# Grid values transposed by TensorE in front of their rescaling, and the split middle chunk of the down projection in two 12-bit parts

## The chip, the cores and the metric

The kernel runs on one core of one Trainium2 chip. The metric is the device time of one execution in microseconds (us). The kernel before takes 656.72 us, the median of three runs (656.42 to 659.26). TensorE (PE) multiplies matrices and transposes, VectorE (DVE), ScalarE (ACT) and GpSimd (POOL) work element by element, and SyncE (SP) issues the DMAs. Each engine takes its instructions in program order and waits for the others on semaphores.

## The reference

The input `x` has 4 batches of 2048 tokens with 256 values. Everything is float32. Per batch:

```python
xn = layernorm(x)
Q, K, V = xn @ Wq.T + bq, xn @ Wk.T + bk, xn @ Wv.T + bv
Q, K = l2_norm(Q), l2_norm(K)                  # over the tokens
tailor = 1 / (L + einsum('bnc,bc->bn', Q, sum(K) + 1e-6))
s = xn + gamma * (sum(V) + Q (K.T V)) * tailor # linear attention
gate, up = q(xn) @ q(w_gate).T, q(xn) @ q(w_up).T
h = silu(gate) * up                            # 704 values per token
g = silu(q(h) @ q(w_down).T)
out = x + s * g
```

`q` is a blockwise 4-bit quantization and its inverse: in each block of 16 neighbouring values the scale is the largest magnitude divided by 6, each value divided by its scale is rounded to the grid 0, 0.5, 1, 1.5, 2, 3, 4, 6 (with sign), and multiplied by the scale again. A grid value fits 16 bits exactly, and a grid value times its scale needs float32.

## The kernel before

**Tiling.** The 8192 tokens are 32 groups of 256. A group lies on 128 partitions with two tokens (`t` = 0, 1) on each. The attention uses that all it needs of a batch is the Gram matrix of `xn` with a column of ones: `gram_step` (L325) adds a group to it, after the eighth group of a batch `attention` turns it into a 256x256 matrix `M`, and `attend` (L509) multiplies each group's transposed tokens with it.

**One group's way through the feed-forward part.** `normalize` (ScalarE, L300) makes `xn`. The blocks' scales are found by VectorE (L152, L161, L165), `over` divides by them (L178), `short` (ScalarE, L211) makes 16-bit patterns and `on_grid` (VectorE, L221) rounds these to the grid. So far the tokens are on the partitions; the matmuls need the features there. So the 16-bit grid values are transposed, and multiplied afterwards by scales that are transposed as well: `turn_scales` transposes the scales of h of one group and of x of another on TensorE (L394), ScalarE evicts them, one DMA writes them to DRAM (`there`) and another reads them back with each scale repeated for its block (`se`, 960 KB). `turn_q` (L413) transposes the grid values, with a DMA from SBUF to SBUF. `rescale_x` (L417) and `rescale_h` (L427) multiply the two into `xqt` and `hqt`. The first five groups of x go another way: they are rescaled first and transposed as float32 by TensorE (`turn_xq`, L362).

`gate_up` (L440) multiplies `xqt` with the gate and up weights, 2 tokens x 3 column chunks; ScalarE evicts the halves (`si`, `up`) and GpSimd multiplies them to `h`. `down` (L467) multiplies `hqt` with `wdt`.

**The 11 chunks of h.** The 1408 values of a partition (704 of each token) are 11 chunks of 128, so that the middle one holds 64 values of the first token and 64 of the second. `down` uses it twice, once for each token, against weights whose other half is zero: 6 + 6 matmuls of 128x128 by 256 columns.

**The order.** It is written out by hand. A loop over `s` = 3 to 30 issues in one step: `gate_up` of group s+1 in three pieces with `gram_step(s+3)` between them, the scales of h of group s-1, `rescale_x(s+2)`, `turn_xn(s+3)`, `down(s-3)`, `turn_scales`, `attend(s-7)`, the grid values of h of group s-1 and x of group s+3 with their `turn_q`, `rescale_h(s-2)`, stores, and `normalize(s+4)`. The attention of a batch is a generator: each `turn()` issues its next piece (L573 and L618 to L693). Behind the loop the last groups are finished with less to put between them. PSUM has eight banks: two `tp` (transposes and the attention), two `gu`, two `od` (down projection and the attention), `at`, `gram`.

**Queues.** All DMAs of a step stand in SP's queue: load of x, reload of x, `there`, `se`, the transposes of h and x, and the store.

Of the kernel before, what the change touches and what calls it, by code (L numbers as in the profile page):

```python
# [8 lines left out]
F32 = mybir.dt.float32  # L9
BF16 = mybir.dt.bfloat16  # L10
F16 = mybir.dt.float16
AF = mybir.ActivationFunctionType
ALU = mybir.AluOpType
# [6 lines left out]
ONE = 2.0**-14  # L20
TO_512 = 2.0**32
DOWN = 1.0 - 3 * 2.0**-24


@with_exitstack
def kernel(
# [22 lines left out]
    nc = tc.nc  # L49
    B, C, L = x.shape  # L50
    FF = w_gate.shape[0]
    P = 128
    T = 2
# [18 lines left out]
    alg = ctx.enter_context(tc.tile_pool(name="alg", bufs=1))  # L72
    ps_tp = ctx.enter_context(tc.tile_pool(name="ps_tp", bufs=2, space=bass.MemoryType.PSUM))
    ps_gu = ctx.enter_context(tc.tile_pool(name="ps_gu", bufs=2, space=bass.MemoryType.PSUM))
    ps_od = ctx.enter_context(tc.tile_pool(name="ps_od", bufs=2, space=bass.MemoryType.PSUM))
    dram = ctx.enter_context(tc.tile_pool(name="dram", bufs=2, space=bass.MemoryType.DRAM))
# [71 lines left out]
    nc.scalar.activation(small.tile([P, 1], F32, tag="warm", name="warm"), ident[:, 0:1], AF.Silu)  # L148

# [215 lines left out]


    scales, spread_sc, turned = {}, {}, {}

# [40 lines left out]

    def turn_q(kind: str, n: int, q: bass.AP):  # L410
        F = q.shape[1]
        qt = tok.tile([P, F // P, P], F16, tag=f"qt{kind}", name=f"qt_{kind}{n}", bufs=2 if kind == "h" else 1)
        nc.sync.dma_start_transpose(qt, q)  # L413
        turned[kind, n] = qt

    def rescale_x(n: int, key: int):
        nc.vector.tensor_tensor(  # L417
            xqt_tile(n),
            turned.pop(("x", n)).rearrange("p g t -> p (g t)"),
            spread_sc[key][:, NIC:, :].rearrange("p g t -> p (g t)"),  # L420
            ALU.mult,
        )

    def rescale_h(n: int):
        ht = tok.tile([P, HF], F32, tag="hqt", name=f"hqt_{n}", bufs=2)
        hqt[n] = ht.rearrange("p (g t) -> p g t", t=P)
        nc.vector.tensor_tensor(  # L427
            ht,
            turned.pop(("h", n)).rearrange("p g t -> p (g t)"),
            spread_sc[n][:, 0:NIC, :].rearrange("p g t -> p (g t)"),  # L430
            ALU.mult,
        )

# [26 lines left out]
    hqt = {}  # L460

    def down(n: int):
        od = ps_od.tile([P, T, L], F32, tag="od", name=f"dn_{n}")
        half = NIC // T
        for t in range(T):
            for i in range(half + 1):
                nc.tensor.matmul(  # L467
                    od[:, t, :],
                    hqt[n][:, t * half + i, :],
                    wdt[:, t * (half + 1) + i, :],  # L470
                    start=(i == 0),
                    stop=(i == half),
                )
        hqt.pop(n)
        return od
# [70 lines left out]
    def attention(b: int):  # L546
# [18 lines left out]
        yield  # L565
        yield
        xs = []
        for i, (pool, tag) in enumerate(
            ((ps_od, "od"), (ps_tp, "tp"), (ps_tp, "tp"), (ps_od, "od"))
        ):  # L570
# [9 lines left out]
            xs.append(ps)  # L580
        yield
        yield
# [62 lines left out]
        for c in range(KC):  # L645
# [6 lines left out]
            )  # L652


        pts = []
        for t in range(KC):
# [9 lines left out]
            pts.append(ps)  # L666
        yield
        yield
# [48 lines left out]

    wdt = const.tile([P, NIC + 1, L], F32, tag="wdt", name="wdt")

    def turn_d(wdz):  # L720
        half = NIC // T
        H = P // 2
        ends = small.tile([P, KC, P], F32, tag="ends", name="ends", bufs=1)
        w3 = wdz.rearrange("p (t f) -> p t f", t=KC)
        nc.scalar.copy(ends[:, :, 0:H], w3[:, :, FF - H : FF])
        nc.scalar.copy(ends[:, :, H:P], w3[:, :, 0:H])
        nc.gpsimd.memset(wdt[H:P, half, :], 0.0)
        nc.gpsimd.memset(wdt[0:H, half + 1, :], 0.0)
        for i in range(0, NIC - 1, 2):
            tp = ps_tp.tile([P, 512], F32, tag="tp", name=f"tp_d{i}")  # L730
            at = [i + k if i + k < half else i + k + 2 for k in range(2)]
            for k in range(2):
                f0 = at[k] * P if at[k] < half else (at[k] - half - 2) * P + H
# [4 lines left out]
            if at[1] == at[0] + 1:  # L738
                evict_over_one(wdt[:, at[0] : at[0] + 2, :].rearrange("p i n -> p (i n)"), tp)
            else:  # L740
                for k in range(2):
                    evict_over_one(wdt[:, at[k], :], tp[:, k * L : (k + 1) * L])
            yield
        tp = ps_tp.tile([P, 512], F32, tag="tp", name="tp_d")
        for t in range(KC):
            nc.tensor.transpose(tp[:, t * P : (t + 1) * P], ends[:, t, :], ident)
        evict_over_one(wdt[0:H, half, :], tp[0:H, 0:L])
        evict_over_one(wdt[H:P, half + 1, :], tp[H:P, 0:L])
        yield
# [104 lines left out]
    turn_xq(4, rounded(s_x, tx))  # L854
    turn_q("h", 0, on_grid(h_state, th))
    gate_up(3, 0, *chunks[1])
# [14 lines left out]
    turn_scales(1)  # L871
    turn_q("h", 1, on_grid(h_state[1], th))
    turn_q("x", 5, on_grid(s_x, tx))
    load_x(9)
    rescale_h(0)
    normalize(6)
    moments = statistics(7, 8)
# [13 lines left out]
    for s in range(3, N - 1):  # L891
# [100 lines left out]
    gate_of(n - 2, od)  # L992
    turn_q("h", n, on_grid(h_state, th))
    rescale_h(n - 1)
    for i in range(4):
# [5 lines left out]
    rescale_h(n)  # L1001
    gate_of(n - 1, od)
# [55 lines left out]
```

## Time and profile before

| | |
|---|---|
| time, median of 3 runs | 656.72 us (656.42 to 659.26) |
| the profiled execution's own time | 656.78 us |
| its span, first to last instruction | 655.0 us |
| TensorE busy | 635.2 us, 97% of the span |
| VectorE, ScalarE, GpSimd busy | 398.1, 286.8, 289.3 us |
| DMA moved | 74.17 MB, mean 113 GB/s |
| DMA transposes | 32 of h (4.65 us median on the queue), 27 of x (4.70 us) |

A row of a group of instructions has the line of the kernel, the engine, the operation, what it writes and reads by the program's names, the shape, the count, then busy time in us and the mean of one in ns, then the engine's idle time just before them and who ended it. A row of the timeline has start and length in us. "PEld" is TensorE's weight load, which overlaps its passes ("PE"). A float32 matmul of the program leaves two loads and two passes in the trace. The lengths of passes hold the drain of the array, and neighbours overlap, so a pass's cost is the distance between two starts. "issue" is time in which an engine waited for nothing that the profile shows.

### The profile page before, as it was taken

The numbers are of one execution on the slowest core, as the hardware profiler recorded it, in microseconds if no ns is written. First come the engines' busy times: TensorE is split into PE (matmuls) and PEld (weight loads), VectorE is DVE, ScalarE is ACT, GpSimd is POOL, SyncE is SP. The second block draws the span as 40 slices with busy tenths as digits, with TensorE's granted clock in tenths as the row PEclk, the third lists the DMA queues.
The fourth block names the chain that finished last, engine by engine and source line by source line (L and its number), as shares of the span: only waits on it lengthen the run. The fifth ranks groups of instructions, "written<-read, shape, count | busy, mean of one in ns | idle before, by whom it ended". The sixth has DMA issues, their size and how long they took to land.

```text
span 655.0 us, 7910 instructions
## 1 busy us (share of the span) xinstructions
PE 635.2 (97%) x2484; PEld 435.2 (66%) x2486; DVE 398.1 (61%) x707; ACT 286.8 (44%) x701; POOL 289.3 (44%) x545
## 2 busy tenths in 40 slices
PE   4899999999999999999999999999999999999997
PEld 2455666666766666667766666776666766666886
DVE  6777584958574555747554565836757554566632
ACT  2557745343444444334534534444444444433230
POOL 5656362452535363172644525264263625336132
PEclk9999999999999999999999999999999999999999
DMA  9200578876778487857488877748868784885882
GB/s 220 90 18 0 74 126 111 108 110 71 113 112 130 122 138 139 142 59 115 116 139 142 112 109 133 113 108 140 134 77 127 114 112 108 123 124 80 143 197 83
DMA packets 86230, 74.17 MB, mean 113 GB/s; under 512 B 64076, under 2 KB 70444, under 8 KB 86188
## 3 DMA queue, kind: packets, MB, share of 16 engines
q1 hardware_dynamic: 85916, 73.40, 67.2%
q8 instruction: 20, 0.33, 0.2%
q10 hardware_dynamic: 272, 0.26, 0.1%
q14 instruction: 22, 0.18, 0.1%
HBM read 48.30 MB, written 10.27 MB: 89 GB/s over the span
## 4 chain that ended last, share of the span: by engine, by line
PE 95%; ACT 2%; DVE 1%; DMA 1%; POOL 1%; issue 0%; SPq 0%; DVEq 0%; ACTq 0%; POOLq 0%
PE gu L440 46%; PE dn L467 25%; PE at L509 8%; PE gram L325 6%; PE px L573 2%; PE tp_xn L342 2%; PE pm L659 1%; PE pa L638 1%; DMA wgu_n<-in_L_ffn_w_up_dram 1%; PE tp_sc L394 1%; PE tp_xq L362 0%; ACT xn L300 0%; PE pM L693 0%; PE pq L623 0%; PE tp_d L735 0%
## 5 line engine op out<-in xcount | busy, mean ns | idle before, releaser
L440 PE MATMUL gu<-wgu,xqt 128*128 128x512 f32 (+1 forms) x768 | 314.1, 557 | 2.2 <-ACT xqt L312 2.2
L453 POOL TENSOR_TENSOR h<-si,up 128x256 f32<-128x256 f32 (+1 forms) x192 | 154.8, 811 | 296.3 <-ACT up L451 296.3
L440 PEld LDWEIGHTS gu<-wgu,xqt 128*128 128x128 f32 x768 | 142.4, 190 | 134.2 <-issue 104.3
L467 PE MATMUL dn<-wdt,hqt 128*128 128x256 f32 x768 | 171.0, 379 | 0.0
L449 ACT ACTIVATE si<-gu 128x256 f32<-128x256 f32 (+1 forms) x192 | 70.7, 368 | 203.0 <-PE gu L440 201.1
L467 PEld LDWEIGHTS dn<-wdt,hqt 128*128 128x128 f32 x768 | 144.1, 190 | 19.0
L417 DVE TENSOR_TENSOR xqt<-qt_x,se 128x512 f32<-128x512 f16 x27 | 25.7, 951 | 153.7 <-DMA qt_x<-t_x 153.7
L451 ACT COPY up<-gu 128x256 f32<-128x256 f32 (+1 forms) x192 | 67.8, 353 | 0.0
L178 DVE SCALAR_TENSOR_TENSOR y_h<-h,inv_h 128x1408 f32<-128x1408 f32 x32 | 57.5, 1796 | 5.9 <-ACT t_h L211 4.9
L325 PEld LDWEIGHTS gram<-xn 128*128 128x128 f32 x256 | 44.2, 194 | 25.3 <-issue 13.2
L509 PE MATMUL at<-M,xnt 128*128 128x256 f32 x256 | 59.7, 379 | 0.0
L427 DVE TENSOR_TENSOR hqt<-qt_h,se 128x1408 f32<-128x1408 f16 x32 | 52.1, 1627 | 8.8 <-DMA qt_h<-t_h 8.8
L325 PE MATMUL gram<-xn 128*128 128x257 f32 (+1 forms) x256 | 48.8, 334 | 7.4 <-ACT xn L300 7.4
L312 ACT ACTIVATE sct<-tp_sc 120x128 f32<-120x128 f32 (+1 forms) x32 | 8.8, 277 | 105.3 <-PE tp_sc L394 105.3
L152 DVE TENSOR_REDUCE scs<-h 128x88 f32<-128x1408 f32 x32 | 51.6, 1613 | 0.0
L509 PEld LDWEIGHTS at<-M,xnt 128*128 128x128 f32 x256 | 46.7, 190 | 6.7
L211 ACT ACTIVATE t_h<-y_h 128x1408 f16<-128x1408 bf16 x32 | 44.5, 1390 | 4.5 <-DVE y_h L178 4.5
L526 POOL TENSOR_TENSOR gate<-gate,xl 128x512 f32<-128x512 f32 x26 | 34.4, 1324 | 21.7 <-DVE gate L519 21.7
L300 ACT ACTIVATE xn<-x,shift,rstd 128x256 f32<-128x256 f32 x64 | 34.9, 598 | 13.7 <-POOL shift L290 13.6
L519 DVE TENSOR_TENSOR gate<-gate,at 128x512 f32<-128x512 f32 x31 | 21.1, 680 | 13.2 <-PE at L509 13.2
L165 DVE RECIPROCAL inv_h<-scs 128x120 f32<-128x120 f32 (+1 forms) x32 | 27.9, 873 | 1.1
L152 DVE TENSOR_REDUCE scs<-xn 128x32 f32<-128x512 f32 x27 | 18.4, 680 | 12.0 <-ACT xn L300 12.0
(132 smaller groups left out, 527.7 us busy)
## 6 DMA issues: line engine op xcount, KB each, us to landing
se<-there SPq DMA_DIRECT2D x27, 960.0 KB
x<-in_L_attn_x_dram SPq DMA_DIRECT2D x32, 256.0 KB
out_dram<-gate SPq DMA_DIRECT2D x31, 256.0 KB
xl<-in_L_attn_x_dram SPq DMA_DIRECT2D x26, 256.0 KB
se<-there SPq DMA_DIRECT2D x5, 704.0 KB
there<-sct SPq DMA_DIRECT2D x27, 60.0 KB
wd_n<-in_L_ffn_w_down_dram SPq DMA_DIRECT2D x1, 704.0 KB
wgu_n<-in_L_ffn_w_up_dram SPq DMA_DIRECT2D x2, 256.0 KB
```

Source lines behind the costliest of these rows:

```text
L152: nc.vector.tensor_reduce(sc, src.rearrange("p a (n k) -> p a n k", k=BLK), AX.X, ALU.max, apply_absolute_value=True)
L178: nc.vector.scalar_tensor_tensor(y.rearrange("p (a n k) -> p a n k", a=a, k=BLK), src.rearrange("p a (n k) -> p a n k", k=BLK), DOWN, inv. ...
L211: nc.scalar.activation(t, upper, AF.Copy, scale=ONE * (1.0 + 2.0**-8))
L300: nc.scalar.activation(xns[n % len(xns)][:, t, 0:L], x_sb[n][:, t, :], AF.Identity, scale=rstd[:, t : t + 1], bias=shift[:, t : t + 1],)
L325: nc.tensor.matmul(grams[b][:, o : o + L + 1 - c * P], xn[:, t, c * P : (c + 1) * P], xn[:, t, c * P : L + 1], start=(g == 0 and t == 0 an ...
L427: nc.vector.tensor_tensor(ht, turned.pop(("h", n)).rearrange("p g t -> p (g t)"), spread_sc[n][:, 0:NIC, :].rearrange("p g t -> p (g t)"), ...
L440: nc.tensor.matmul(gu[:, : nb * P], xqt[n][:, t, c, :], wgu[:, c, j0 * P : (j0 + nb) * P], start=(c == 0), stop=(c == KC - 1),)
L449: nc.scalar.activation(si[:, :nb, :], pair[:, :, 0, :], AF.Silu)
L451: nc.scalar.copy(up[:, :nb, :], pair[:, :, 1, :])
L453: nc.gpsimd.tensor_tensor(hs[n][:, o : o + nb * 64], si[:, :nb, :].rearrange("p j f -> p (j f)"), up[:, :nb, :].rearrange("p j f -> p (j f)"),
L467: nc.tensor.matmul(od[:, t, :], hqt[n][:, t * half + i, :], wdt[:, t * (half + 1) + i, :], start=(i == 0), stop=(i == half),)
L509: nc.tensor.matmul(ready[n][:, t, :], xt[:, c, t * P : (t + 1) * P], M[:, c, :], start=False, stop=(c == KC - 1), skip_group_check=True,)
```

## The change

There are two parts, and what they need.

**Transposes on TensorE.** `turn_q` goes. `on_grid`'s result is kept, and `turn_chunks`, called by `rescale_x` and `rescale_h`, transposes it on TensorE where it is about to be rescaled: as bfloat16 patterns, against a bfloat16 identity, up to 8 chunks into one PSUM bank. VectorE then reads the bank as float16. `rescale_h` becomes two instructions, of 8 and of 3 chunks. So the transposes of h of group s-2 stand at the end of step s on TensorE, behind `attend(s-7)`, and those of x of group s+2 behind the third piece of `gate_up`. `tp` gets three banks, `od` one; the attention's px and pa take `tp` banks for `od` ones, and some of its `yield`s move.

**The middle chunk.** `part_middle` makes, for each token, a stationary matrix `both` whose one half of the partitions holds the token's 64 values with 12 significant bits (a ScalarE copy, scaled by just under 1, into float32r) and whose other half holds what this leaves of them. `down` multiplies each with two weight matrices `wde` of float32r, the weights' upper part and what it leaves, both stacked twice over the partitions. It has 5 float32 matmuls and 2 float32r matmuls for each token then. `turn_d` prepares `wde`, once. The subtractions are done by GpSimd in the loop and by VectorE for the last groups. The last `attend` but one moves ahead of the last `down`.

```diff
-    ps_tp = ctx.enter_context(tc.tile_pool(name="ps_tp", bufs=2, space=bass.MemoryType.PSUM))
+    ps_tp = ctx.enter_context(tc.tile_pool(name="ps_tp", bufs=3, space=bass.MemoryType.PSUM))
...
-    ps_od = ctx.enter_context(tc.tile_pool(name="ps_od", bufs=2, space=bass.MemoryType.PSUM))
+    ps_od = ctx.enter_context(tc.tile_pool(name="ps_od", bufs=1, space=bass.MemoryType.PSUM))
...
+    ident16 = const.tile([P, P], BF16, tag="ident16", name="ident16")
+    nc.scalar.copy(ident16, ident)
...
-    def turn_q(kind: str, n: int, q: bass.AP):
-        F = q.shape[1]
-        qt = tok.tile([P, F // P, P], F16, tag=f"qt{kind}", name=f"qt_{kind}{n}", bufs=2 if kind == "h" else 1)
-        nc.sync.dma_start_transpose(qt, q)
-        turned[kind, n] = qt
+    def turn_chunks(q: bass.AP, g0: int, g1: int, nm: str) -> bass.AP:
+        tp = ps_tp.tile([P, 1024], BF16, tag="tp", name=f"tp_q{nm}_{g0}")
+        for g in range(g0, g1):
+            o = (g - g0) * P
+            nc.tensor.transpose(tp[:, o : o + P], q[:, g * P : (g + 1) * P].bitcast(BF16), ident16)
+        return tp[:, 0 : (g1 - g0) * P].bitcast(F16)
...
-            turned.pop(("x", n)).rearrange("p g t -> p (g t)"),
+            turn_chunks(turned.pop(("x", n)), 0, T * KC, f"x{n}"),
...
+        q = turned.pop(("h", n))
+        for g0, g1 in ((0, 8), (8, NIC)):
+            cols = slice(g0 * P, g1 * P)
+            nc.vector.tensor_tensor(
+                ht[:, cols],
+                turn_chunks(q, g0, g1, f"h{n}"),
+                spread_sc[n][:, g0:g1, :].rearrange("p g t -> p (g t)"),
+                ALU.mult,
+            )
...
+    def part_middle(n: int, engine):
+        H = P // 2
+        middle = hqt[n][:, NIC // T, :]
+        both = tok.tile([P, T, P], F32R, tag="both", name=f"both_{n}", bufs=2)
+        sides = slice(0, H), slice(H, P)
+        for t in range(T):
+            nc.scalar.activation(both[sides[t], t, :], middle[sides[t], :], AF.Copy, scale=SHORT)
+        for t in range(T):
+            engine.tensor_tensor(
+                both[sides[1 - t], t, :],
+                middle[sides[t], :],
+                both[sides[t], t, :].bitcast(F32),
+                ALU.subtract,
+            )
+        over_lower[n] = both
...
         for t in range(T):
-            for i in range(half + 1):
+            for i in range(half):
                 nc.tensor.matmul(
                     od[:, t, :],
-                    hqt[n][:, t * half + i, :],
-                    wdt[:, t * (half + 1) + i, :],
+                    hqt[n][:, t * (half + 1) + i, :],
+                    wdt[:, t * half + i, :],
...
+            for k in range(2):
+                nc.tensor.matmul(
+                    od[:, t, :],
+                    both[:, t, :],
+                    wde[:, k, t, :],
...
-            ((ps_od, "od"), (ps_tp, "tp"), (ps_tp, "tp"), (ps_od, "od"))
+            ((ps_od, "od"), (ps_tp, "tp"), (ps_tp, "tp"), (ps_tp, "tp"))
...
-        ps = ps_od.tile([P, KC, L], F32, tag="od", name=f"pa_{b}")
+        ps = ps_tp.tile([P, KC, L], F32, tag="tp", name=f"pa_{b}")
...
+        nc.scalar.activation(wde[:, 0], all_ends, AF.Copy, scale=SHORT)
+        nc.gpsimd.tensor_tensor(wde[:, 1], all_ends, wde[:, 0].bitcast(F32), ALU.subtract)
...
-            turn_q("h", h, on_grid(h_state, th))
+            turned["h", h] = on_grid(h_state, th)
...
-            turn_q("x", s + 3, on_grid(s_x, tx))
+            turned["x", s + 3] = on_grid(s_x, tx)
...
                 rescale_h(h)
+        part_middle(s - 2, nc.gpsimd if s < N - 2 else nc.vector)
...
+    rescale_h(n - 2)
+    part_middle(n - 2, nc.vector)
     gate_of(n - 3, od)
-    rescale_h(n - 2)
...
+    attend(n - 1)
     od = down(n)
     gate_of(n, od)
-    attend(n - 1)
```

More of the change, by code (lines that the diff above doesn't have):

```diff
@@ L11 @@
 F16 = mybir.dt.float16
+F32R = mybir.dt.float32r
 AF = mybir.ActivationFunctionType
@@ L21 @@
 TO_512 = 2.0**32
+SHORT = 1.0 - 2.0**-13
 DOWN = 1.0 - 3 * 2.0**-24
@@ L147 @@
         xns.append(xn)
-    nc.scalar.activation(small.tile([P, 1], F32, tag="warm", name="warm"), ident[:, 0:1], AF.Silu)
+    nc.scalar.activation(small.tile([P, 1], F32, tag="warm", name="warm", bufs=1), ident[:, 0:1], AF.Silu)
     def largest(sc: bass.AP, src: bass.AP):
@@ L426, in rescale_h @@
         hqt[n] = ht.rearrange("p (g t) -> p g t", t=P)
[L427 to L432, printed above, removed]
+        q = turned.pop(("h", n))
[7 more added lines that the diff above has]
+            )
     def gate_up(n: int, t: int, j0: int, nb: int):
@@ L460 @@
     hqt = {}
+    over_lower = {}
+    def part_middle(n: int, engine):
[13 more added lines that the diff above has]
+        over_lower[n] = both
     def down(n: int):
@@ L464, in down @@
         half = NIC // T
+        both = over_lower.pop(n)
         for t in range(T):
-            for i in range(half + 1):
+            for i in range(half):
                 nc.tensor.matmul(
                     od[:, t, :],
-                    hqt[n][:, t * half + i, :],
-                    wdt[:, t * (half + 1) + i, :],
+                    hqt[n][:, t * (half + 1) + i, :],
+                    wdt[:, t * half + i, :],
                     start=(i == 0),
-                    stop=(i == half),
+                    stop=False,
+                    skip_group_check=True,
+                )
+            for k in range(2):
[3 more added lines that the diff above has]
+                    wde[:, k, t, :],
+                    start=False,
+                    stop=(k == 1),
+                    skip_group_check=True,
                 )
@@ L566, in attention @@
         yield
+        yield
         xs = []
         for i, (pool, tag) in enumerate(
-            ((ps_od, "od"), (ps_tp, "tp"), (ps_tp, "tp"), (ps_od, "od"))
+            ((ps_od, "od"), (ps_tp, "tp"), (ps_tp, "tp"), (ps_tp, "tp"))
         ):
@@ L580, in attention @@
             xs.append(ps)
-        yield
         yield
@@ L652, in attention @@
             )
+        yield
         pts = []
@@ L666, in attention @@
             pts.append(ps)
-        yield
         yield
@@ L715, in turn_gu @@
             evict_over_one(wgu[:, c, j0 * P : (j0 + nb) * P], tp[:, : nb * P])
-    wdt = const.tile([P, NIC + 1, L], F32, tag="wdt", name="wdt")
+    wdt = const.tile([P, NIC - 1, L], F32, tag="wdt", name="wdt")
+    wde = const.tile([P, 2, T, L], F32R, tag="wde", name="wde")
     def turn_d(wdz):
@@ L722, in turn_d @@
         H = P // 2
-        ends = small.tile([P, KC, P], F32, tag="ends", name="ends", bufs=1)
         w3 = wdz.rearrange("p (t f) -> p t f", t=KC)
[L725 to L728, printed above, removed]
         for i in range(0, NIC - 1, 2):
             tp = ps_tp.tile([P, 512], F32, tag="tp", name=f"tp_d{i}")
-            at = [i + k if i + k < half else i + k + 2 for k in range(2)]
             for k in range(2):
-                f0 = at[k] * P if at[k] < half else (at[k] - half - 2) * P + H
+                f0 = (i + k) * P if i + k < half else (i + k - half) * P + H
                 for t in range(KC):
@@ L737, in turn_d @@
                     )
[L738 to L742, printed above, removed]
+            evict_over_one(wdt[:, i : i + 2, :].rearrange("p i n -> p (i n)"), tp)
             yield
         tp = ps_tp.tile([P, 512], F32, tag="tp", name="tp_d")
[L745 to L748, printed above, removed]
+        for k, f0 in enumerate((FF - H, 0)):
+            ends = small.tile([P, KC, P], F32, tag="ends", name=f"ends_{k}", bufs=1)
+            for o in (0, H):
+                nc.scalar.copy(ends[:, :, o : o + H], w3[:, :, f0 : f0 + H])
+            for t in range(KC):
+                nc.tensor.transpose(tp[:, k * L + t * P : k * L + (t + 1) * P], ends[:, t, :], ident)
+        all_ends = alg.tile([P, KC, L], F32, tag="G1", name="all_ends")
+        evict_over_one(all_ends.rearrange("p k n -> p (k n)"), tp)
+        nc.scalar.activation(wde[:, 0], all_ends, AF.Copy, scale=SHORT)
+        nc.gpsimd.tensor_tensor(wde[:, 1], all_ends, wde[:, 0].bitcast(F32), ALU.subtract)
         yield
@@ L854 @@
     turn_xq(4, rounded(s_x, tx))
-    turn_q("h", 0, on_grid(h_state, th))
+    turned["h", 0] = on_grid(h_state, th)
     gate_up(3, 0, *chunks[1])
@@ L871 @@
     turn_scales(1)
-    turn_q("h", 1, on_grid(h_state[1], th))
-    turn_q("x", 5, on_grid(s_x, tx))
+    turned["h", 1] = on_grid(h_state[1], th)
+    turned["x", 5] = on_grid(s_x, tx)
     load_x(9)
     rescale_h(0)
+    part_middle(0, nc.gpsimd)
     normalize(6)
@@ L992 @@
     gate_of(n - 2, od)
-    turn_q("h", n, on_grid(h_state, th))
+    turned["h", n] = on_grid(h_state, th)
     rescale_h(n - 1)
+    part_middle(n - 1, nc.vector)
     for i in range(4):
@@ L1001 @@
     rescale_h(n)
+    part_middle(n, nc.vector)
     gate_of(n - 1, od)
```

## The prediction, made before the changed kernel was run

> **What bounds the kernel now.** I read the page's busy times first, then busy times in chosen stretches, the chain that ended last, one step of the timeline, the waits of TensorE, and last the groups by shape. The busy row puts TensorE at 97%, but a busy matmul row says nothing of who waits, so the stretches come next (after the stretch and its length: PE, PEld, DVE, ACT, POOL busy, granted clock, DMA share, GB/s):
>
> ```profile
> PE 635.2 (97%) x2484; PEld 435.2 (66%) x2486; DVE 398.1 (61%) x707; ACT 286.8 (44%) x701; POOL 289.3 (44%) x545
> ...
> 0.00:72.00 72.00, 57.87 (x222) 34.33 (x224) 51.05 (x107) 38.78 (x89) 40.27 (x107) 1.00 0.28 75
> 72.00:107.00 35.00, 35.00 (x134) 22.02 (x133) 22.60 (x32) 20.36 (x54) 18.29 (x30) 1.00 0.87 121
> ...
> 330.00:574.00 244.00, 243.48 (x943) 166.69 (x942) 144.10 (x239) 107.47 (x268) 107.48 (x188) 1.00 0.73 119
> ...
> 650.50:655.00 4.50, 0.00 (x0) 0.00 (x0) 1.60 (x4) 0.00 (x0) 0.36 (x1) 0.81 0.33 117
> ```
>
> TensorE's idle time is 72 - 57.9 = 14.1 us before the first DMA transpose is even issued (72.6 us), 4.5 us behind its last matmul, and about 1 us in the 578 us between. There it is a queue without holes at granted clock 1.00: what is added to it lengthens the span one for one, what is removed shortens it. One step in order (start, length, instruction):
>
> ```profile
> 226.88 3.60 PE L440 MATMUL gu<-wgu,xqt 128*128 128x512 f32 x8
> 230.31 1.48 PE L325 MATMUL gram<-xn 128*128 128x257 f32 x8
> 231.62 6.18 PE L440 MATMUL gu<-wgu,xqt 128*128 128x512 f32 x16
> 237.64 0.60 PE L342 MATMUL tp_xn<-ident,xn 128*128 128x128 f32 x4
> 238.07 5.34 PE L467 MATMUL dn<-wdt,hqt 128*128 128x256 f32 x24
> 243.25 0.27 PE L394 MATMUL tp_sc<-ident,scs 128*120 128x128 f32 x1
> 243.36 1.89 PE L509 MATMUL at<-M,xnt 128*128 128x256 f32 x8
> 245.09 1.45 PE L440 MATMUL gu<-wgu,xqt 128*128 128x512 f32 x3
> ```
>
> Lengths include the drain, so I take differences of starts. A step is 18.21 us. The 24 passes of the down projection take 243.25 - 238.07 = 5.18 us, 216 ns each; a program f32 matmul leaves two passes (12 matmuls, x24), so one costs 432 ns. Four f32 transposes take 238.07 - 237.64 = 0.43 us, 108 ns each.
>
> The waits that the change removes are VectorE's (us in total, times, the longest):
>
> ```profile
> DVE xqt L417 <- DMA qt_x<-t_x: 153.7, 26, 8.7
> ...
> DVE hqt L427 <- DMA qt_h<-t_h: 8.8, 3, 3.8
> ```
>
> They look large and are worth nothing: in the step above VectorE is busy 10.6 of 18.2 us and nothing on TensorE waits for it.
>
> **The change, part by part.** All is summed on the profiled execution: span 655.0, 1.78 us around it, 656.78 us; the median shown is 656.72, so no correction is needed.
>
> (1) The DMA transposes go: 32 of h and 27 of x, some 4.7 us each on SP's queue. Loads, stores and the spread scales `se` behind them move up. Worth 0, since TensorE waited for none.
>
> (2) TensorE gets their work: 11 chunks for each of 32 groups and 4 for each of 27, 352 + 108 = 460 transposes of 16-bit patterns, each a weight load and a 128-column pass. No row shows one; the nearest are these:
>
> ```profile
> 620.40 0.59 PE L491 MATMUL zero_gu<-zero 128*128 128x512 bf16 x2
> 620.83 5.34 PE L467 MATMUL dn<-wdt,hqt 128*128 128x256 f32 x24
> ...
> L491 PEld LDWEIGHTS <-zero x4: 98/98/105, 2.0 to 620.4; 128*128 128x128 bf16 x4
> ...
> L467 PEld LDWEIGHTS dn<-wdt,hqt 128*128 128x128 f32 x768 | 144.1, 190 | 19.0
> L342 PEld LDWEIGHTS tp_xn<-ident,xn 128*128 128x128 f32 x128 | 16.1, 144 | 7.8 <-issue 4.2 <-ACT wgu L312 0.3
> ```
>
> Two 512-column bf16 passes take 620.83 - 620.40 = 0.43 us, 0.42 ns a column, so 128 columns need 54 ns: the lower bound. The upper is the f32 transpose, 108 ns. The load decides between them. Its record is latency and streaming: f32 takes 190 ns, an f32 transpose's 144, bf16's 98, and in the f32 runs the 190 hide behind passes started 108 ns apart. The shorter bf16 load should hide too, so I stay near the streaming end: 62 ns, 460 x 0.062 = +28.5 us (24.8 to 49.7). The Trainium skill, page "TensorE: Matmul & The Clock Gate", section "Back-to-back issue gap", speaks against me: alternating loads and 128-column matmuls sustain about 81 ns. By that rule the term is 37.3 us. The f32 transposes beside it keep their pure streaming pace with a load before each, so I follow the row; 81 stays within the range. After each of the 59 runs one f32 weight load, with up to 108 ns known to be enough, has only 54 ns of cover: up to 54 ns x 59 = 3.2 us, I take +1.5.
>
> (3) The down projection: 12 f32 matmuls a group become 10 and 4 float32r ones (two per half, stacked parts). Removed 2 x 432 = 864 ns a group. A float32r pass of 256 columns is in no row. If it is one pass at one column per cycle it costs 256 x 0.42 = 108 ns. The Trainium skill, "FP8 and Floating Point Precision", section "TensorE Precision Notes", gives true FP32 four passes and a reduced form that reads four bytes and truncates: a quarter of 432, also 108. A row here speaks against it: the f32 transpose is one recorded pass, and still takes 108 ns for 128 columns, twice the two-byte pace. By that row 256 columns cost 216 and the four 864, no gain. I take 108, because a transpose must carry all 32 bits through and a truncated operand need not: 32 x (864 - 432) = -13.8 us. Ends: -13.8 and, as full f32, 32 x (4 x 432 - 864) = +27.6.
>
> (4) The parts (L482 to L489): two ScalarE scalings and two subtractions of 64x128 per group, on GpSimd, in the last four groups on VectorE. ScalarE's nearest row is the 120x128 eviction, 0.28 us: 0.5 us of 18.2, with ScalarE busy 8. GpSimd's nearest row is its 128x192 multiply, 0.69, taken half: 0.7 us, with GpSimd busy 8 to 10. Hidden; the down projection reads them 11 us later.
>
> (5) Moved waits. `rescale_h` stood at 241.24 in the step, before; it now needs the transposes at the step's end. Queued behind it on VectorE: statistics (2.3 us, every second step), scales and `y_h` (1.61 + 0.68 + 0.22 + 0.91 + 1.62 = 5.0), `gate`, `y_x`. Counting from the next step's first matmul: first half (1024 of 1408 elements of 1.61 us, an estimate of 1.2) from -0.2 to 1.0, second to 1.6, statistics to 3.9, `y_h` to 8.9. ScalarE asked for `y_h` at 235.85 - 226.88 = 9.0 before: just in time, and late would delay evictions whose bank is next wanted at 18. On ScalarE the first scaling waits for the half done at 1.0; behind it stands `normalize` (1.1), done at 1.0 + 0.5 + 1.1 = 2.6, and the Gram step wants it at 3.4. Cover 0.8 us; each further tenth would cost TensorE 2.7 us over 27 steps. On TensorE the h transposes wait for `rescale_x` to free a bank (12 against 17 us), and `se`, asked for a step earlier, no longer shares the queue. I take 0.
>
> (6) Banks: `od` has one buffer. In steps its eviction follows at once and the next use is 13 us off: 0. At the end it shows: `down(n-2)` comes right behind its own transposes, and waits for the first half (1.2), two scalings (0.5) and the Silu of the previous bank (0.6), 2.3 us, less three transposes and three zeroing passes (0.84): +1.5. Start-up: two more f32 transposes, +0.2; the third `tp` buffer can remove little, since the short waits of TensorE for evictions of `tp` add up to 3.3 us.
>
> Sum: 28.5 + 1.5 - 13.8 + 0.2 + 1.5 = +17.9, so 656.78 + 17.9 = **674.7 us**, 2.7% slower.
>
> **Rivals.** A, the float32r passes run at the four-byte pace: 674.7 + 13.8 = 688.5 (716 if as full f32, "12-bit parts" then saving nothing). For: the f32 transposes' pace. Against: the four-pass count. B, the weight load paces the 16-bit transposes, 108 ns each: +49.7 - 13.8 + 1.7 gives 694.4. For: every one has a load and 54 ns to hide it. Against: f32 loads hide. C, the 0.8 us of cover in front of the Gram step is gone, by 0.5 us a step: 674.7 + 13.5 = 688. For: four engines hand over in a row there. Against: VectorE and ScalarE half idle. D, faster: the transposes slip under weight loads and cost TensorE nearly nothing. The change pays once a transpose is below (13.8 - 1.7) / 460 = 26 ns; at 18 ns it gives 656.8 + 8.3 - 12.1 = 653. Against: half the streaming time of 128 columns in any row. Even float32r passes at no cost would save 27.6 and only break even.
>
> **Chances.** The likeliest 0.62 (54 to 81 ns, float32r at 108: 669 to 684), A 0.17, B 0.11, C 0.07, D 0.03. A run of this kernel tells 0.5%, 3.3 us, from no change. Low end: streaming pace, no exposed load, no stall at the end, a microsecond of start-up, 656.8 + 24.8 - 13.8 - 1 = 667. High end: just over B, 696, which also holds A and C. Left out: D, full f32, and mixtures of A with B, below 0.2. Faster 0.03, same 0.02, slower 0.95.
>
> **What would show it.** Groups by shape: `tp_q` x460 with starts some 60 ns apart; float32r rows, 128 passes, 108 ns apart; the 20 remaining f32 passes of a group at 216. A plain step grows from 18.2 to about 18.8 us. VectorE's wait for `qt_x` becomes a wait for TensorE. No new TensorE wait over 0.3 us a step. It is wrong if TensorE waits for `xn` or VectorE in the steps, or if either new row is off its pace.

## The result and the profile after

The changed kernel takes 680.97 us, the median of four runs (677.92 to 682.29), against 656.73 us (656.42 to 659.26) for the kernel before: a ratio of 1.035, 95% interval 1.031 to 1.040. It is slower, as predicted, by 24.2 us where 17.9 were forecast; 680.97 lies inside the range of 667 to 696. The profiled execution took 681.94 us with a span of 680.0, so 25.0 us of span are to be explained (680.0 - 655.0).

First the busy row of the page of the changed kernel (engine, busy us, share of the span, instructions):

```profile
PE 655.7 (96%) x2946; PEld 454.2 (67%) x2948; DVE 411.8 (61%) x747; ACT 308.6 (45%) x768; POOL 284.8 (42%) x600
```

TensorE is busy for 20.5 us more, and for a point less of a longer span: 4.5 of the 25 us are new idle time. The same kernel's busy times by stretch tell where (stretch, its length, then PE, PEld, DVE, ACT, POOL, granted clock, DMA share, GB/s):

```profile
72.00:86.00 14.00, 12.23 (x53) 8.02 (x52) 6.76 (x17) 9.62 (x25) 5.26 (x8) 0.88 0.20 55
143.00:166.00 23.00, 21.00 (x98) 14.73 (x97) 13.79 (x29) 9.08 (x23) 5.81 (x8) 1.00 0.33 69
330.00:590.00 260.00, 259.61 (x1181) 180.21 (x1179) 154.91 (x256) 120.33 (x306) 111.97 (x232) 1.00 0.38 90
632.00:676.00 44.00, 41.43 (x223) 35.38 (x222) 21.80 (x40) 12.99 (x25) 10.15 (x8) 0.96 0.31 100
```

The long middle is a queue without holes, as before: 259.6 of 260 us, at full clock, with the DMA share down to 0.38 from 0.73. The three other stretches have holes of about 2 us each that the kernel before did not have there, and in the first and the last the granted clock is below 1. So there are two kinds of cost, one per step and one at single places. The starts of the Gram steps, which stand in every kernel at the same place of a step, divide the span into three (us; the last column is the profiled span):

| | start to 7th Gram step | 7th to 32nd Gram step | 32nd to the end | span |
|---|---|---|---|---|
| before | 82.4 | 475.7 | 96.9 | 655.0 |
| after | 85.5 (+3.1) | 492.0 (+16.3) | 102.5 (+5.6) | 680.0 |

**A plain step.** TensorE's timeline of one step of the changed kernel (start, length, instruction), from the first pass of the gate and up projection to that of the next step:

```profile
199.16 3.65 PE L449 MATMUL gu<-wgu,xqt 128*128 128x512 f32 x8
...
209.98 0.39 PE L419 MATMUL tp_qx<-ident,t_x 128*128 128x128 bf16 x4
210.20 0.61 PE L346 MATMUL tp_xn<-ident,xn 128*128 128x128 f32 x4
210.65 2.32 PE L498 MATMUL dn<-wdt,hqt 128*128 128x256 f32 x10
212.62 0.58 PE L507 MATMUL dn<-wde,both 128*128 128x256 f32 x2
...
215.44 0.27 PE L399 MATMUL tp_sc<-ident,scs 128*120 128x128 f32 x1
...
217.27 0.78 PE L419 MATMUL tp_qh<-ident,t_h 128*128 128x128 bf16 x11
217.89 2.36 PE L449 MATMUL gu<-wgu,xqt 128*128 128x512 f32 x5
```

The step takes 217.89 - 199.16 = 18.73 us (before 18.21; 18.8 forecast). Four transposes of x take 210.20 - 209.98 = 0.22 us and eleven of h 217.89 - 217.27 = 0.62: 56 ns each. The down projection takes 215.44 - 210.65 = 4.79 us instead of 5.18. The split into the two kinds of pass can't be read from the starts of the first rows, because a float32r record begins before the pass ahead of it has ended; the chain of the same kernel, below, has modelled stretches without overlap: 2.16 us for ten float32 passes and 0.24 or 0.23 for two float32r ones. With 216 ns for a float32 pass, as before, the four float32r passes of a group take 4.79 - 20 x 0.216 = 0.47 us, 118 ns each. Transposes at 15 x 56 = +0.84 and the parts at -0.39 leave +0.07 for the two exposed weight loads of a step.

**The attention's wait.** The chain that ended last of the changed kernel, where it runs through an attention (start, length, what):

```profile
132.04 2.16 PE dn L498 x10
134.20 0.24 PE dn L507 x2
...
138.95 11.70 DMA se<-there
...
150.73 0.70 DVE xqt L423
...
151.48 1.99 PE pa L679 x8
```

`pa` waits on TensorE for VectorE's rescaling of x, although it reads nothing of it: with `pa` moved into the `tp` banks it takes the bank that the x transposes of this step had, and this is free only once `rescale_x` has read it. `rescale_x` itself waits for its scales, `se`, which land 11.7 us after their issue. The waits of TensorE and of VectorE in the changed kernel (engine, instruction, who ended the wait: us in total, times, the longest):

```profile
PE pa L679 <- DVE xqt L423: 2.2, 3, 1.8
PE tp_d L783 <- ACT ends L781: 1.7, 2, 1.1
PE dn L498 <- ACT gate L520: 1.7, 1, 1.7
PE pm L701 <- DVE hqt L436: 0.9, 4, 0.2
```

```profile
DVE hqt L436 <- PE tp_qh L419: 129.1, 27, 6.6
DVE xqt L423 <- DMA se<-there: 39.0, 16, 5.4
```

VectorE's long waits for the DMA transposes have become waits for TensorE and for `se`. Most of them cost as little; the four lines of TensorE, 6.5 us, are the new holes. Some older and shorter waits of TensorE for `tp` banks are gone, so its idle time grows by 4.5 only. The longest of those that are gone (waits of TensorE, kernel before):

```profile
PE tp_xq L362 <- ACT wgu L312: 1.4, 1, 1.4
...
PE pb_u L541 <- ACT sct L312: 1.0, 4, 0.3
```

The 25 intervals between the 7th and the 32nd Gram step show the same, from starts alone. Twenty of them are 0.50 to 0.61 us longer than before. Three, in which `pa` and `pm` run, are 3.03, 1.53 and 1.43 us longer, which is 4.4 us over the 0.52 of a plain step. That is more than the 2.2 and 0.9 of the two lines above, because the waits there are counted from the end of the record before, drain included: the first `pa` has 1.8 us of wait, and starts 1.9 us later behind `pb_r` than in the kernel before. Two, with one of the waits of `pb_u` that are gone, are only 0.02 and 0.04 longer, which is 1.0 us under it. So 25 x 0.52 + 4.4 - 1.0 = 16.4 against the 16.3 of the table.

**Start and end.** The chain of the changed kernel in the start-up, with the two-microsecond stretches of the same place behind it (columns as above, the clock third from the end):

```profile
75.88 0.41 ACT ends L781 x2
76.33 0.45 PE tp_d L783 x2
76.86 0.51 ACT ends L781 x2
77.41 0.44 PE tp_d L783 x2
77.85 2.49 PE gram L329 x8
```

```profile
76.00:78.00 2.00, 1.03 (x6) 0.70 (x7) 0.00 (x0) 0.89 (x5) 0.54 (x1) 0.95 0.04 8
78.00:80.00 2.00, 2.00 (x8) 1.72 (x7) 0.30 (x1) 1.63 (x3) 0.78 (x1) 0.50 0.00 0
```

The weight blocks at the end of the middle chunk (`ends`) have one buffer, so ScalarE's second pair of copies waits for the transposes of the first pair, and these for the copies: 1.7 us of TensorE idle. Right behind it TensorE runs at half clock for 3.4 us (from 77.8 to 81.2 us in rows of one and of half a microsecond): the Gram step takes 2.49 us instead of 1.31. The end looks alike (chain of the changed kernel):

```profile
641.23 1.24 DVE hqt L436
...
643.15 0.61 ACT gate L520
643.81 4.07 PE dn L498 x10
```

This is the stall forecast in (6), handover by handover, and behind it ten passes take 4.07 us instead of 2.16.

### The profile page after: what moved, and what is told of

It reads as the page before. It is cut to its first block, busy times and chain, and to the rows that moved or that the text cites. A ratio compares the mean times of both kernels' runs of the same rounds, so it can differ in the third digit from the quotient of the medians.

```text
span 680.0 us, 8900 instructions
## 1 busy us (share of the span) xinstructions
PE 655.7 (96%) x2946; PEld 454.2 (67%) x2948; DVE 411.8 (61%) x747; ACT 308.6 (45%) x768; POOL 284.8 (42%) x600
## 2 busy tenths in 40 slices
DMA packets 25465, 59.14 MB, mean 87 GB/s; under 512 B 3308, under 2 KB 9676, under 8 KB 25420
## 4 chain that ended last, share of the span: by engine, by line
PE 88%; DMA 6%; DVE 2%; ACT 2%; issue 1%; POOL 1%; DVEq 0%; ACTq 0%; SPq 0%
PE gu L449 41%; PE dn L498 20%; PE at L550 8%; PE gram L329 6%; DMA se<-there 5%; PE tp_qh L419 2%; PE dn L507 2%; PE px L615 2%; PE tp_xn L346 2%; PE pa L679 1%; DVE hqt L436 1%; PE tp_qx L419 1%; PE pm L701 1%; PE zero_at L538 1%; PE tp_sc L399 1%
## 5 line engine op out<-in xcount | busy, mean ns | idle before, releaser
L462 POOL TENSOR_TENSOR h<-si,up 128x256 f32<-128x256 f32 (+1 forms) x192 | 143.2, 753 | 186.7 <-ACT up L460 186.1
L498 PE MATMUL dn<-wdt,hqt 128*128 128x256 f32 x640 | 150.4, 382 | 1.7 <-ACT gate L520 1.7
L436 DVE TENSOR_TENSOR hqt<-tp_qh,se 128x1024 f32<-128x1024 f16 x64 | 54.0, 886 | 145.7 <-PE tp_qh L419 129.1
L498 PEld LDWEIGHTS dn<-wdt,hqt 128*128 128x128 f32 x640 | 118.2, 191 | 16.2 <-ACT gate L520 2.2
L484 POOL TENSOR_TENSOR both<-hqt,both 64x128 fp32r<-64x128 f32 x56 | 25.3, 451 | 133.0 <-ACT both L482 130.6
L182 DVE SCALAR_TENSOR_TENSOR y_h<-h,inv_h 128x1408 f32<-128x1408 f32 x32 | 53.9, 1685 | 2.2 <-ACT t_h L215 1.1
L423 DVE TENSOR_TENSOR xqt<-tp_qx,se 128x512 f32<-128x512 f16 x27 | 18.7, 691 | 60.0 <-DMA se<-there 39.0
L482 ACT ACTIVATE both<-hqt 64x128 fp32r<-64x128 f32 x64 | 19.7, 308 | 72.1 <-DVE hqt L436 71.3
L507 PE MATMUL dn<-wde,both 128*128 128x256 f32 x128 | 37.8, 376 | 0.0
```

The source lines that it names most:

```text
L182: nc.vector.scalar_tensor_tensor(y.rearrange("p (a n k) -> p a n k", a=a, k=BLK), src.rearrange("p a (n k) -> p a n k", k=BLK), DOWN, inv. ...
L436: nc.vector.tensor_tensor(ht[:, cols], turn_chunks(q, g0, g1, f"h{n}"), spread_sc[n][:, g0:g1, :].rearrange("p g t -> p (g t)"), ALU.mult,)
L462: nc.gpsimd.tensor_tensor(hs[n][:, o : o + nb * 64], si[:, :nb, :].rearrange("p j f -> p (j f)"), up[:, :nb, :].rearrange("p j f -> p (j f)"),
L498: nc.tensor.matmul(od[:, t, :], hqt[n][:, t * (half + 1) + i, :], wdt[:, t * half + i, :], start=(i == 0), stop=False, skip_group_check=True,)
L507: nc.tensor.matmul(od[:, t, :], both[:, t, :], wde[:, k, t, :], start=False, stop=(k == 1), skip_group_check=True,)
```

## The experiments

**One part alone.** The first run leaves the down projection and its weights as they were, and the second leaves the transposes on the DMA queue and the banks as they were (shortened to the sense of the edits):

```diff
# transposes only
-    part_middle(...)                     # and both, wde, all_ends
-            for i in range(half):
+            for i in range(half + 1):
# parts only
-            turn_chunks(q, g0, g1, f"h{n}"),
+            turned.pop(("h", n)).rearrange("p g t -> p (g t)"),   # by turn_q; x alike
-    tp: bufs=3, od: bufs=1
+    tp: bufs=2, od: bufs=2
```

> The change's first part alone: transposes on TensorE, the down projection as before with 12 float32 matmuls a group. My theory: the 460 transposes cost 56 ns each (25.8 us with a little for exposed loads, 27) and the float32r parts had saved 32 x 0.39 = 12.5 us. So this kernel is 12.5 us above the changed one, less the start-up stall that the weights' extra preparation made and the slow clock behind it (1.7 + 1.9 us): about 690 us, 33 above the kernel before. Rival A (float32r saves nothing): at most 681 us, like the changed kernel.

> The change's second part alone: DMA transposes, two od banks and two tp banks as before, the middle chunk in 12-bit parts. My theory: a plain step falls from 18.21 to 17.82 us, 32 x 0.39 = 12.5 us less on TensorE, perhaps 2 to 4 us of it lost again at the start where TensorE waits for the copies of the weights' ends: 644 to 648 us, faster than both kernels. Rival A (float32r at the four-byte pace): 656 to 660 us. A second rival: the DMA transposes come late and the parts need them, then TensorE waits for the subtraction in the steps and the gain is lost.

Transposes alone: 686.9 us (686.75 to 687.33), ratio 1.045 (1.043 to 1.048), near the 690 and far from rival A's 681. (The expectation left out that the stall at the end and the half clock behind it, 1.7 + 1.9 us, are not in this kernel either; without them it is 3 us lower.) Parts alone: 652.21 us (650.36 to 654.67), ratio 0.993 (0.990 to 0.995): a gain, but 4 us above the upper end of what was expected. Together they give 686.9 + 652.2 - 656.7 = 682.4, against 681.0 to 681.5 measured for both. Their stalls at the start and the end differ, so part of this agreement is luck; in a plain step, where there are none, the two add up. TensorE's waits in the profile of transposes alone:

```profile
PE pa L653 <- DVE xqt L423: 2.2, 3, 1.4
PE pm L675 <- DVE hqt L436: 0.9, 4, 0.2
```

The waits for `pa` and `pm` are the same without the parts, so they belong to the transposes and the banks. A plain step takes 19.12 us here, +0.91: (56 x 15 + 2 x 35) ns. With the -0.38 of the parts alone (17.83 us) this gives the +0.52 of both. The 460 transposes ran at a granted clock of 0.999 to 1.0 in all four runs, so they did not slow the clock. With parts alone TensorE is busy for 625.0 us instead of 635.2; the 10.2 us don't all arrive, because of these (waits of TensorE, then chain, of parts alone):

```profile
PE dn L488 <- DVE hqt L429: 3.0, 1, 3.0
PE tp_d L772 <- ACT ends L770: 1.7, 2, 1.1
```

```profile
624.86 10.47 DMA qt_h<-t_h
...
637.10 2.42 PE dn L488 x10
```

The stall for `ends` comes with the parts. And the last DMA transpose of h, 10.5 us from issue to landing, comes too late for the last down projection: 3.0 us. In the kernel before, TensorE reached this projection 13.0 us after the issue of the transpose (641.83 - 628.85); here it would be there after 9.3, so it waits. In this run that is the one place where a DMA transpose costs TensorE time.

**The waits taken away.** In the changed kernel, `pb_r` and `pa` are issued one turn later, when `rescale_x` has read the bank, each pair of `ends` gets its own buffer and is copied early, and `gate_of(n - 3)` stands ahead of `rescale_h(n - 2)`, so that the Silu doesn't queue behind the two scalings:

```diff
         yield
+        yield
         r_b = alg.tile([P, L], F32, tag="row", name=f"rb_{b}", bufs=2)
...
+            if i in (0, 4):
+                ends = small.tile([P, KC, P], F32, tag="ends", name=f"ends_{i}", bufs=2)
...
+    gate_of(n - 3, od)
     rescale_h(n - 2)
     part_middle(n - 2, nc.vector)
-    gate_of(n - 3, od)
```

> The changed kernel with three waits of TensorE taken away by order and buffers: the attention's pb_r and pa one turn later, so that pa's bank is not the one that rescale_x frees; the copies of the weights' ends made earlier into two buffers; at the end the Silu of the previous od bank ahead of the two scalings. My theory (the miss against the forecast is waits, 2.2 us at pa, 1.7 at the start, 0.6 of 1.9 at the end, and the slow clock behind the last two, up to 3.8): 673 to 675 us. Rival (the late scales only move their wait to another place): 678 us or more, with a new TensorE wait for rescale_x or rescale_h in the trace.

It took 673.43 us (673.08 to 674.32), ratio 1.025 (1.022 to 1.027), at a clock of 0.999 to 1.0 in every run. So 7.5 to 8 of the 24 us are waits and what comes with them. They did not vanish altogether (waits of TensorE, this run):

```profile
PE pm L701 <- DVE hqt L436: 1.3, 4, 0.6
PE pm L701 <- DVE G L688: 0.8, 1, 0.8
PE dn L498 <- DVE hqt L436: 0.5, 1, 0.5
```

`pa` is free, and `pm`, the next in the same banks, waits a little more instead. By the three stretches of the table this run stands 0.9 us ahead of the kernel before at the 7th Gram step, +14.7 in the steps and +2.6 behind them.

To part the wait of `pa` from the others, one run moves `pa` alone, and the changed kernel ran once more beside it:

> The changed kernel with pb_r and pa alone one turn later. My theory: TensorE's wait for rescale_x, three times up to 1.9 us, is gone and nothing comes in its place: 2 to 4 us less than the unchanged one beside it. Rival (the late scales are needed anyway): no difference, the wait shows in front of the next step's gate_up.

> The changed kernel again, unchanged, beside the two others on one chip, since runs of it lie at 677.9, 680.0, 681.9 and 682.3 us with granted clocks of 1.000, 0.997, 0.994 and 0.994. Theory idle: each stretch of half clock costs about 2 us, so the runs should lie on such steps again: 678, 680, 682. Theory late scales: the wait in front of pa differs from run to run, 2 to 4 us in all, whatever the clock.

`pa` one turn later: 676.46 us (676.39 to 676.95), ratio 1.029 (1.027 to 1.031). The changed kernel again: 681.49 (678.71 to 682.77), ratio 1.036 (1.034 to 1.039). So 5.0 us came back, more than the 2 to 4 expected. In the profiles of these two runs (spans of 679.5 and 675.0) it is 1.4 us up to the 7th Gram step, 1.5 in the steps and 1.6 behind them. The 1.5 is what moving `pa` gives, since the waits of `pm` grew to 1.3 and 0.8. The rest is clock: all four runs with `pa` moved had 0.999, although the other stalls, the 1.7 us for `ends` and the 1.7 for `gate`, are still in the profile, and neither is followed by half clock there. The changed kernel had 0.993 to 0.996 in four of five runs, and in its fifth, at 0.999, took 678.71. Its first four runs order in the same way: 677.92 us at 1.000, 679.99 at 0.997, 681.94 and 682.29 at 0.994. One stretch at half clock costs about 2 us, and the changed kernel mostly has two. The wait in front of `pa` was 2.1 us here, as in the first profile, so the runs' spread is not that of late scales.

**Is it the idle time that slows the clock?** Matmuls of zeros that compute nothing that is used fill the two places: four and two in front of the two pairs of `ends`, eight in front of `down(n - 2)`; the rest is the changed kernel.

```diff
+            keep_busy(4 if k == 0 else 2)
             for t in range(KC):
                 nc.tensor.transpose(tp[:, k * L + t * P : k * L + (t + 1) * P], ends[:, t, :], ident)
...
+    for _ in range(8):
+        nc.tensor.matmul(opened["gu"], zero[:, 0:P], zero, start=True, stop=True)
     od = down(n - 2)
```

> The changed kernel with zero matmuls issued in the two idle stretches in front of which the granted clock halves: 4 and 2 passes of 512 columns ahead of the transposes of the weights' ends, 8 ahead of down(n-2) at the end; their results are not used and all waits stay. Theory idle (TensorE's idle time makes the clock fall): granted clock 1.00 throughout, 3 to 4 us less, 677 to 678 us. Theory transposes (16-bit transposes make it fall): the slow stretches stay, 681 us.

It took 681.07 us (680.15 to 682.0), ratio 1.036: a miss, by 3 us. In its profile the two places run at full clock and the time is not better for it (chain at the end, then a wait of TensorE):

```profile
641.98 1.73 PE zero_gu L1026 x8
643.70 2.38 PE dn L498 x10
```

```profile
PE pa L679 <- DVE xqt L423: 3.7, 3, 1.9
```

The ten passes behind the filled gap take 2.38 us instead of 4.07, and the stretch from 72 to 86 us has a clock of 1.00. Against the profile of the changed kernel this is 1.6 us less up to the 7th Gram step and 1.8 less behind the 32nd, but 1.5 more between them, where `pa` waited for 3.7 us instead of 2.2. And two of the four runs had a clock of 0.997 and 682 us; where these lost it is not known.

Does idle time make the clock fall? The run does not show it: with `pa` alone moved, the same two places kept the full clock without being filled. The profiles of all eleven runs do show, in rows of one microsecond, where the clock falls while TensorE has work: six times, for 3.4 us each, and each time right behind an idle time of TensorE. These are the two places of the changed kernel, in both its profiles; the place of `ends` with the parts alone; and one in the start-up of the last run below, behind 2.7 us of idle time. It never falls where the queue is full. But idle times of the same size also pass without it: both places with `pa` moved, the 3.0 us at the end with the parts alone, and the start of the kernel before. So an idle time of 1.7 us or more can bring a half-clock stretch and need not; what decides stays open. The rival in the expectation, that 16-bit transposes slow the clock, falls by the run with the transposes alone (above), and two of the six stretches lie in kernels with DMA transposes.

The Trainium skill, page "TensorE: Matmul & The Clock Gate", section "What's actually happening", has a gate that passes half or all of the clock, decided over windows of about 3.4 us that run freely. The 0.50 in the stretch above and the six times 3.4 us agree with it, and windows that fall differently across the same gap would let it pass in one run and not in another. In one thing the case differs: the page has the clock fall after at least one idle window of about 3.4 us, and here it fell behind 1.7. No run here sets the phase of the windows, and the first gap, at 76 us, lies ahead of everything that moving `pa` changes, so why its four runs all kept the clock is not explained.

**A version from the better half.** Parts alone gain, so the next run keeps the DMA transposes and takes the stalls away: `ends` copied early into one buffer, the last group's h transposed by TensorE (11 transposes, where the DMA was late), and the last `attend` but one ahead of the last `down`.

```diff
-    turn_q("h", n, on_grid(h_state, th))
+    turned["h", n] = on_grid(h_state, th)
...
-    rescale_h(n)
+    rescale_h_here(n)      # turn_chunks on TensorE, for this group only
...
+    attend(n - 1)
     od = down(n)
...
-    attend(n - 1)
```

> The second part alone, with its two stalls taken away: the copies of the weights' ends made earlier into a buffer for both, and the h of the very last group, whose DMA transpose came 3.0 us late for its down projection, turned by TensorE (11 transposes of 56 ns); the last attend but one ahead of the last down. My theory: the whole gain of the parts on TensorE shows, 656.7 - 12.5 + 0.8 = 645 us, range 643.5 to 647, granted clock 1.00. Rival (something else takes the gain of the steps, the copies and subtractions on ScalarE and GpSimd for example): 650 us or more as in the second part alone.

It took 647.86 us (646.94 to 649.41), ratio 0.986 (0.984 to 0.989), 0.9 us above the range expected. Its chain shows a further hole in the start-up, the second place where a DMA transpose costs time:

```profile
72.57 8.41 DMA qt_h<-t_h
...
83.40 0.61 ACT xn L304
84.05 1.58 PE gram L329 x8
```

`part_middle(0)` stands on ScalarE ahead of `normalize(6)`, and waits for the first DMA transpose; the Gram step gets its `xn` late by 1.3 us. The next run exchanges these two lines, and nothing else:

```diff
     rescale_h(0)
-    part_middle(0, nc.gpsimd)
     normalize(6)
+    part_middle(0, nc.gpsimd)
```

> The version with the parts alone, the end blocks copied early and the last group turned by TensorE, with one more line moved: in front of the loop part_middle(0) stands behind normalize(6) on ScalarE, so that normalize(6) no longer waits for the DMA transpose of the first group of h. The whole reference is computed. If ScalarE's order is what holds the Gram step there, TensorE's wait of 9.8 us for xn (8.1 at its longest, some of it in the start where the first groups of x arrive anyway) falls by what the transpose and the rescaling last beyond normalize: the version without this move took 647.9, so 645.5 to 646.5. If TensorE only goes on to wait for what stands behind (the down projection of group 0 needs the same transpose, but a step later, or statistics on VectorE behind rescale_h), it stays at 647.5 to 648. Rival of the clock: a stretch at half clock there, at 647 or more with a mean granted clock below 0.998.

645.86 us (645.13 to 648.21), ratio 0.984 (0.981 to 0.986), as expected; in its profile the 7th Gram step starts at 82.34 us instead of 84.05. The last run gives it the changed kernel's banks as well:

> The version with normalize(6) moved, and on top of it only the changed kernel's bank division: three tp banks and one od bank, with px and pa of the attention in tp and its yields as in the change. DMA transposes stay, so no rescaling holds a tp bank for long. The whole reference is computed. The prediction held that the third tp bank can remove little. Theory: in the profiles with three banks the seventh Gram step's predecessors run 1.8 to 2.4 us earlier in the start (with the transposes on TensorE alone the sixth Gram step starts at 74.75 us, before at 77.12), so 645.9 - 1.8 to 2.4 = 643.5 to 644.1, if the single od bank stalls nothing. Rival: the earlier start came from the DMA transposes' absence or the order in front, then it stays at 645.5 to 646.2; or the single od bank makes a down projection or px wait once a batch, then 646 to 648.

645.53 us (643.79 to 646.38), ratio 0.981 (0.979 to 0.984): by its time not to be told from the one without. The profiles tell them apart (TensorE's waits of this run, then its timeline in the start-up, then the same Gram steps of the run without the banks):

```profile
PE gu L464 <- ACT xqt L316: 4.3, 3, 2.7
...
PE px L627 <- ACT gate L532: 1.0, 1, 1.0
PE dn L510 <- ACT gate L532: 0.6, 1, 0.6
```

```profile
19.76 5.40 PE L464 MATMUL gu<-wgu,xqt 128*128 128x512 f32 x8 [2.74 <-ACT xqt L316]
25.00 1.48 PE L329 MATMUL gram<-xn 128*128 128x257 f32 x8
...
77.58 1.48 PE L329 MATMUL gram<-xn 128*128 128x257 f32 x8
```

```profile
23.07 1.48 PE L329 MATMUL gram<-xn 128*128 128x257 f32 x8
...
77.04 1.48 PE L329 MATMUL gram<-xn 128*128 128x257 f32 x8
```

The profiled execution met a half-clock stretch in its first 25 us: the first eight passes of `gu` come after an idle time of 2.74 us and take 5.40 us instead of 3.70, so the second Gram step is 1.9 us late. From there to the sixth it needs 77.58 - 25.00 = 52.6 us, against 77.04 - 23.07 = 54.0 without the banks. So the third `tp` bank is worth 1.4 us in the start-up, and the late beginning hid it. The same stretch takes 53.8 us in the kernel before and 52.4 with the transposes alone, which has three `tp` banks too. That is most of the 1.8 and 2.4 us by which the changed kernel, and the transposes alone, are ahead of the kernel before just ahead of the sixth Gram step; the rest, 0.4 and 1.0, is a difference in the first 23 us, where the profiles of all runs vary. The waits for `pb_u` are gone as well, and the single `od` bank costs 1.6 (`px` and `dn`). And `pa`, which is in a `tp` bank here, does not wait: the bank division alone is not what makes it wait.

## Why the prediction was right in sign and short in size

The sign and the main mechanism hold: TensorE is a full queue, the transposes were taken from a resource that it did not wait for and put into it, and the parts give back less than half. Its steps:

| step | forecast | measured | from |
|---|---|---|---|
| (1) DMA transposes gone | 0 | 0 in the steps | middle stretch full before and after |
| (2) 460 transposes | 62 ns, +28.5 | 56 ns, +25.8 | starts in a step |
| (2) exposed loads | +1.5 | 35 ns x 59, +2.1 | 0.07 a step |
| (3) float32r passes | 108 ns, -13.8 | 118 ns, -12.5 | 32 x -0.39 |
| (4) making the parts | 0 | 0 in the steps | steps of 18.73 |
| (5) moved waits | 0 | +3.4 | three steps 4.4, two -1.0 |
| (6) start-up | +0.2 | +2.5 | 3.1 less the 0.6 of eleven transposes |
| (6) end, stall | +1.5 | +1.7 | `dn` waits for `gate` |
| end, half clock | none | +1.9 | 4.07 instead of 2.16 us |
| sum | +17.9 | +24.9 | of 25.0 in the span |

**(1), (2), (4) held.** The DMA traffic fell from 74.17 to 59.14 MB, and no time came of it. The choice in (2) to follow the float32 transposes' row and not the rule of the Trainium skill, page "TensorE: Matmul & The Clock Gate", section "Back-to-back issue gap" (about 81 ns for a load and a 128-column pass, which gives an estimate of 37.3) was right, and could have gone further: 56 ns is streaming time with next to nothing on top. A load of a new matrix before every pass hides behind 54 ns of cover. Rivals B and D fall by this number.

**(3) held in mechanism, its size was off by a tenth.** A float32r pass does not go at the pace of the float32 transpose, by which it would have been 216; rival A falls. The estimate from the four passes that the Trainium skill, page "FP8 and Floating Point Precision", section "TensorE Precision Notes", gives true FP32 was 108, the trace has 118. The records show 2 passes in 0.23 to 0.24 us; what takes the 10 ns is not shown.

**(5) is the step that failed, at "I take 0".** I followed the banks for the h transposes ("wait for `rescale_x` to free a bank (12 against 17 us)") and not for the attention, whose `pa` the change moves from `od` into the same `tp` rotation. Three times it arrives before `rescale_x` lets go of the bank, once by 1.8 us. I also had `se` arrive earlier, since the queue is shorter. It lands 11.7 us after its issue in the chain above, and VectorE waits for it 16 times, 39 us in total. The waits of `pa` and `pm` are in the kernels with the transposes and in none without them, not even in the one with the changed banks, and moving `pa` removes its own: shown. So 3.4 us stand where the prediction has 0, and one of its own signs of being wrong, TensorE waiting for VectorE in the steps, came true. The handover in front of the Gram step, rival C, did not bite: no wait of TensorE for `xn` in the steps.

**(6) foresaw the end and missed the start.** The end stall is the one forecast, 1.7 for 1.5. In the start-up I counted the instructions (two more transposes) and not that `ends` has a single buffer, which makes a chain of copy, transpose, copy, transpose out of them: 1.7 us, in both kernels with the parts, gone when the copies are early. The 2.5 us of the table are this wait, some 1.9 of half clock and 0.7 of instructions and handovers, less the 1.8 that the changed kernel was ahead before them. I let the third `tp` bank "remove little", and it removed 1.4 of these 1.8 us, and the 1.0 of `pb_u` in the steps: most of the 3.3 that the prediction had summed itself.

**No term for the clock.** In the profile both stalls were followed by 3.4 us at half clock, some 1.9 us each. No duration in the trace of before gives this term, though the spread of the kernel before's own runs (656.42 to 659.26 us; in later series 656.4 us at a clock of 0.999 and 658.5 at 0.996) was a hint of its size. It goes with the difference between 677.9 and 682 us among the changed kernel's own runs. With a clock of 1.000 the forecast misses by 3.2 us, about what step (5) left out. That the other errors (-2.7 and +0.6 in (2), +1.3 in (3), +0.4 and +0.2 in (6)) cancel to about zero is luck.

## What to carry to other kernels

Where a tile moves to another pool, follow the rotation of that pool through every user, also the rare ones: the wait appears at the next tile that gets the bank, which reads none of the data. Work that an idle resource did for nothing is not free when it is put into the queue that bounds the kernel; here the half of the change that shortened this queue was worth 11 us by itself, once its own short stalls were moved. A new stall of a microsecond or two on a full TensorE can cost twice that, since the granted clock may fall behind it (here 1.7 us of idle time and 1.9 of half clock, twice).

## What the hardware showed beyond the forecast

A 16-bit transpose of 128x128 with its own weight load takes 56 ns in a run of 4 to 11. A float32r pass of 256 columns takes 118 ns, and a float32 pass 216, with two of these to a matmul. A stretch at half clock lasted 3.4 us in all six cases that the profiles hold, and cost about 1.9 us in the two of the changed kernel; each of the six came right behind an idle time of TensorE (1.7 to 2.7 us), and idle times of this size also passed without one. After the DMA transposes had left the queue, the 960 KB of spread scales still took 11.7 to 11.9 us from issue to landing at the three places where the chain goes through them; how long they took before is not in the traces.
